# An attention and non-local block in float32: the non-local part of image 6 moved behind the last attention, with other first loads, score banks and tail

One core of a Trainium2 chip. The metric is the device time of one execution in microseconds (us), of the slowest core (here the only one); lower is better. A span in a profile is 1.7 us shorter than the device time of the same run. All runs named here are of the fast state.

## The reference, cut

For each of 8 images x of 512 channels and 32 x 32 = 1024 positions, in float32:

```python
# layer 0: attention, 8 heads of d = 64
q, k, v = (conv1x1(x, W, b).reshape(B, 8, 64, 1024) for W, b in (q, k, v))
attn = softmax(einsum('bhdn,bhdm->bhnm', q, k) * 64 ** -0.5)
x = x + conv1x1(einsum('bhnm,bhdm->bhdn', attn, v).reshape(B, 512, 32, 32), Wp, bp)
# layer 1: non-local block with 256 inner channels, then a norm over the whole batch
g, theta, phi = (conv1x1(x, W, b).reshape(B, 256, 1024) for W, b in (g, theta, phi))
y = einsum('bcd,bdn->bcn', einsum('bcn,bdn->bcd', theta, phi) / 1024, g)
z = conv1x1(y, W_w, W_b) + x
z_hat = (z - mean(z, (0, 2, 3))) * rsqrt(var(z, (0, 2, 3)) + 1e-5)
return z_hat * gamma + beta
```

The norm's mean runs over all images, so no output can be stored before the last z of its channels is known.

## The kernel before

Each image goes through the same stages on TensorE, and their names are those of the PSUM tiles in the profile: pq, pv, pk (projections), ps and po (attention: scores and weighted values), den (softmax denominators), pp (projection of the output), ptp (theta and phi), pf (f = theta phi), pg (g), pwf (f folded into W_w) and pz. The large products are done as seven products of half size (Strassen-Winograd), so they need sums of quarters first: t1 to t4 of the data, w3 to w6 of the weights, on VectorE. The stages overlap, so pq, pv and pk of image b + 1 run between the attention of b and its pp.

PSUM has four slots of two banks; the text calls a slot a bank, as the code does. `free` holds their order. The helpers `pe` and `dve` keep an instruction in program order; a scheduler places everything else, DMA issues too.

```python
    free = ["s0", "s1", "s2", "s3"]
    def next_bank(name):
        free.append(free.pop(0))
        return bank(free[-1], name)

    xt = xp.tile([P, CC, N], F32, tag="x", name="x_0")
    load_w(nc.scalar)                          # quarters of WqT, 256 KB each, on ScalarE's queue
    for h in range(NH):
        for k in range(2):                     # x of image 0 in four pieces of 512 KB
            at = slice(k * CC // 2, (k + 1) * CC // 2), slice(h * 512, (h + 1) * 512)
            nc.sync.dma_start(xt[:, at[0], at[1]], x_v[0, :, at[0], at[1]])

    def join_bias(w):                          # bp += Wp bv, once
        for oc in range(CC):
            m, mc = divmod(oc, CC // 2)
            ps = next_bank(f"pbp_{oc}")
            for c in range(CC):
                ...                            # quarter of Wp
                pe(nc.tensor.matmul(ps[:, 0, :1], quarter[...], bv[:, c:c + 1], ...))
            nc.vector.tensor_tensor(bp[:, oc:oc + 1], bp[:, oc:oc + 1], ps[:, 0, :1], ALU.add)
```

The attention takes 64 steps: 8 units (a pair of heads, half of the positions) of 8 blocks of keys. The weighted values follow the scores by LAG = 2 steps. `acc` sums a unit's exponentials; after four units the four `acc` are spread over one tile by DMA (`spread`), VectorE sums it, one product per half gives the denominators, and their reciprocals go through DRAM (`den_d`) to be broadcast back (`r`). In the last image nothing follows the attention behind which this chain could run, so its units 4 to 7 had a product and a reciprocal each (`normalize_alone`).

```python
        def scores(i):
            ps = bank(tags[i % 2], f"ps_{b}_{u}_{m}")
            ...                                # 4 products, then e = exp(scale * ps) on ScalarE
            if m == NB - 1 and u not in alone: # alone: units 4..7 of the last image
                spread(u)
        def denominators(g, ps):
            columns(ps, folds, lambda j: t[:, 0, j * 512:(j + 1) * 512])
            nc.vector.reciprocal(ri, ps)
            nc.sync.dma_start(d, ri)           # den_d
        def normalize(g, d):
            for i in range(4):
                for j in range(2):
                    nc.sync.dma_start(r[j * D:(j + 1) * D, :], d[row, :].partition_broadcast(D))
                dve(nc.vector.tensor_tensor(part(4 * g + i), part(4 * g + i), r, ALU.mult))
        def normalize_alone(u, ps):
            columns(ps, ones, lambda j: acc[:, j, :])
            nc.vector.reciprocal(ri, ps)
            nc.vector.tensor_tensor(part(u), part(u), ri, ALU.mult)
```

The z of images 0 to 4 wait in DRAM (`spill`). In the last image they are read back (`reload`) while TensorE still works.

Of the kernel before, what the change touches and what calls it, by code (L numbers as in the profile page):

```python
# [16 lines left out]
P = 128  # L17
# [13 lines left out]
def unshifted(ctx: ExitStack, tc: tile.TileContext, a: dict, out: bass.AP):  # L31
# [11 lines left out]
    LATE = 3  # L43
    LAG = 2
# [86 lines left out]
    def weights(name):  # L131

        n, w = loaded.pop(0)
        assert n == name
        if name not in kept:
            weight_sums(w, corner[name])
            kept[name] = dram.tile(list(w.shape), F32, tag=f"kept_{name}", name=f"kept_{name}")
            nc.sync.dma_start(kept[name], w)
        return w

    def join_bias(w):

        for oc in range(CC):
            m, mc = divmod(oc, CC // 2)
            ps = next_bank(f"pbp_{oc}")
            for c in range(CC):
                k, kc = divmod(c, CC // 2)
                quarter = {(0, 0): w[:, 0], (0, 1): w[:, 1], (1, 0): corner["WpT"], (1, 1): w[:, 2]}[m, k]
                pe(nc.tensor.matmul(ps[:, 0, :1], quarter[:, kc, mc * P:(mc + 1) * P], bv[:, c:c + 1],
                                    start=(c == 0), stop=(c == CC - 1)))  # L150
            nc.vector.tensor_tensor(bp[:, oc:oc + 1], bp[:, oc:oc + 1], ps[:, 0, :1], ALU.add)  # L151

    def data_sums(quarters, name, width=2):

        b11, b12, b21, b22 = quarters
        t = [block(f"t{i}_{name}")[:, :width, :] for i in range(4)]
        nc.vector.tensor_tensor(t[0], b12, b11, ALU.subtract)
        nc.vector.tensor_tensor(t[1], b22, t[0], ALU.subtract)
        nc.vector.tensor_tensor(t[2], b22, b12, ALU.subtract)
        nc.vector.tensor_tensor(t[3], b21, t[1], ALU.subtract)  # L160
        return {"11": b11, "21": b21, "22": b22, "t1": t[0], "t2": t[1], "t3": t[2], "t4": t[3]}
# [13 lines left out]
    def seven(name, w, data, positions_out, first, add, between=None, early=False):  # L175



        nk, half = w.shape[2], w.shape[3]
        tags = list(free)  # L180
        free[:] = [tags[3], tags[1], tags[0], tags[2]] if early else [tags[3], tags[1], tags[2], tags[0]]
        slots, begun = {}, set()
        for n, (what, wi, di, s, reads) in enumerate(EARLY if early else SEVEN):
            if s not in slots or early and what == "t4":
                slots[s] = bank(tags[s], f"{name}_{s}_{n}")
                begun -= {one for one in begun if one[0] == s}
            ps, d = slots[s], data[di]
            if positions_out:
                parts = [(ps.rearrange("p h (i f) -> p (h i) f", f=half)[:, i, :], i * half // 512,
                          lambda k, i=i: d[:, k, i * P:(i + 1) * P], lambda k: w[:, wi, k, :])  # L190
                         for i in range(512 // P)]
            else:
                parts = [(ps[:, m, :], m, lambda k, m=m: w[:, wi, k, m * P:(m + 1) * P], lambda k: d[:, k, :])
                         for m in range(half // P)]
            for to_ps, at, lhsT, rhs in parts:
                for k in range(nk):
                    pe(nc.tensor.matmul(to_ps, lhsT(k), rhs(k), start=(s, at) not in begun, stop=(k == nk - 1),  # L197
                                        skip_group_check=True))
                    begun.add((s, at))
            for to, is_first in reads:  # L200
                (first if is_first else add)(to, ps)
            if between and n in between:
                between[n]()
# [15 lines left out]
    load_w(nc.scalar)  # L219
    for h in range(NH):  # L220
        for k in range(2):
            at = slice(k * CC // 2, (k + 1) * CC // 2), slice(h * 512, (h + 1) * 512)
            nc.sync.dma_start(xt[:, at[0], at[1]], x_v[0, :, at[0], at[1]])
# [3 lines left out]
    ones = const.tile([P, D], F32, tag="ones", name="ones")  # L227
# [23 lines left out]
    def heads_of(b, what, w, bias, data, **how):  # L251
# [13 lines left out]
        for c in range(CC):  # L265
            nc.vector.tensor_reduce(peak[:, c:c + 1], t[:, c, :], AX.X, ALU.max, apply_absolute_value=True)
# [30 lines left out]
    def attention(b, q, k, v, near_end):  # L297
# [7 lines left out]
        o = mats.tile([P, CC, N], F32, tag="o", name=f"o_{b}")  # L305
        units = [(p, h) for p in range(NPAIR) for h in range(NH)]
        steps = [(u, m) for u in range(len(units)) for m in range(NB)]
        es, accs, sums, folded = {}, {}, {}, {}
        alone = range(4, 8) if b == B - 1 else ()
        tags = list(free)  # L310

        def part(u):
            p, h = units[u]
            return o[:, p, h * 512:(h + 1) * 512]

        def scores(i):
            u, m = steps[i]
            p, h = units[u]
            ps = bank(tags[i % 2], f"ps_{b}_{u}_{m}")
# [14 lines left out]
            if m == NB - 1 and u not in alone:  # L334
                spread(u)

        def weighted(i):
# [10 lines left out]
            if m == NB - 1:  # L348
                nc.scalar.copy(part(u), ps[:, 0, :])
                nc.vector.tensor_tensor(part(u), part(u), ps[:, 1, :], ALU.add)  # L350

        def spread(u):
# [7 lines left out]
            if i == 3:  # L360
# [3 lines left out]
                for to, l, r in ((t[:, 0], t[:, 0], t[:, 1]), (t[:, 2], t[:, 2], t[:, 3]),  # L364
                                 (folded[g][:, 0], t[:, 0], t[:, 2])):
                    nc.vector.tensor_tensor(to, l, r, ALU.add)
# [11 lines left out]
        def normalize(g, d):  # L378
            for i in range(4):
# [6 lines left out]
        def normalize_alone(u, ps):  # L386
            acc = accs.pop(u)
            columns(ps, ones, lambda j: acc[:, j, :])
            ri = w2.tile([P, 512], F32, tag="ri", name=f"ri_{b}_{u}")
            nc.vector.reciprocal(ri, ps)  # L390
            nc.vector.tensor_tensor(part(u), part(u), ri, ALU.mult)

        for i in range(len(steps) + LAG):
            if i < len(steps):
                scores(i)
            if i == len(steps) - 2:
                near_end()
            if i >= LAG:
                weighted(i - LAG)
            if alone and i in (46, 54, 62):  # L400
                ps = bank(tags[3 - i // 8 % 2], f"psum_{i}")
                if i == 46:
                    d = denominators(0, ps[:, 1, :])
                normalize_alone(i // 8 - 1, ps[:, 0, :])
            if alone and i == 58:
                normalize(0, d)
        free[:] = tags
        if not alone:
            return o, denominators, normalize
        normalize_alone(7, next_bank("psum_7")[:, 0, :])  # L410
        return o, None, None

# [26 lines left out]
    def nonlocal_(b, xt, data, tp, wg, before_wf):  # L439
# [3 lines left out]
        f = w2.tile([P, IC, CI], F32, tag="ri", name=f"f_{b}")  # L443

        def make_f():
            ps = next_bank(f"pf_{b}")[:, 0, :].rearrange("p (c d) -> p c d", c=IC)
            for c in range(IC):
                for i in range(NB):
                    pe(nc.tensor.matmul(ps[:, c, :], tp[:, i, c * P:(c + 1) * P], tp[:, i, CI:],  # L449
                                        start=(i == 0), stop=(i == NB - 1)))  # L450
            nc.scalar.mul(f, ps, 1.0 / N)
# [4 lines left out]
        def first(q, ps):  # L456
            d = int(q[0]) - 1
            nc.scalar.activation(part(q), ps[:, 0, :], AF.Identity, bias=gb[:, d:d + 1])  # L458

        seven(f"pg_{b}", wg, data, False, first,  # L460
              lambda q, ps: nc.vector.tensor_tensor(part(q), part(q), ps[:, 0, :], ALU.add), {5: make_f})
# [74 lines left out]
    def last_z():  # L536
        order = [B - LATE, B - 1, *range(B - LATE + 1, B - 1)]
        begun = None
        for oc in range(CC):
            for n, b in enumerate(order):  # L540
                _, g, wf = late[b]
                ps = next_bank(f"pz_{b}_{oc}")
                for h in range(NH):
                    for d in range(IC):
                        pe(nc.tensor.matmul(ps[:, h, :], wf[:, d, oc * P:(oc + 1) * P], g[d][:, h * 512:(h + 1) * 512],  # L545
                                            start=(d == 0), stop=(d == IC - 1)))
                t = z[b][oc]
                dve(nc.vector.scalar_tensor_tensor(t, ps.rearrange("p h n -> p (h n)"), wb[:, oc:oc + 1], t,
                                                   ALU.add, ALU.add))
                if n == 0 and begun:  # L550
                    finish(oc - 1, *begun)
                for h in range(NH):
                    dve(nc.vector.bn_stats(stats[:, oc, b * NH + h, :], t[:, h * 512:(h + 1) * 512]))
# [24 lines left out]
    data = data_sums(quarters_of(xt), "x_0")  # L578
    q, peak_q = heads_of(0, "q", weights("WqT"), bq, data, early=True)
# [9 lines left out]
    load_w(nc.sync)  # L589
    for b in range(B):  # L590
# [5 lines left out]
        def near_end():  # L596
            if not last:
                nxt["data"] = data_sums(quarters_of(nxt["x"]), f"x_{b + 1}")

        o, denominators, normalize = attention(b, q, k, v, near_end)  # L600
# [12 lines left out]
        else:  # L613
            for i, tag in enumerate("vqk"):
# [26 lines left out]
        nonlocal_(b, xt, data, tp, weights("WgT"), before_wf)  # L641
        load_w(nc.sync)
        if b in spill_g:
            put_away(b)
# [8 lines left out]
    pe(nc.tensor.matmul(ps[:D, :1], ones, good, start=True, stop=True))  # L653
# [213 lines left out]
```

## Time and profile before

| | before |
|---|---|
| device time, 3 runs | 2209.64 us (2209.11 to 2211.08) |
| the profiled run | 2211.32 us, span 2209.6 |
| start of pk of image 0 | 33.2 |
| join_bias to pp, pp to ptp (image 0) | 5.87, 27.13 |
| attention of images 0 to 6, first ps to next pq | 110.54 to 110.59 each |
| pk to pp in images 2 to 5 / 1 / 6 | 24.03 / 24.48 / 24.79 |
| ptp of image 6 to ptp of image 7 | 201.07 |
| last product (count) to the end of the span | 22.1 |

The rows below the third are differences between the starts of a stage's first matmul in TensorE's timeline. This is the way in which all gains below are counted: it takes in waits, cold clock and switching alike. The views themselves stand in the prediction. One more serves as the base of a later comparison, the start of an attention (image 2) in TensorE's timeline (columns: start, duration, engine, line, operation, count, and idle time before it):

```profile
627.55 1.95 PE L324 MATMUL ps<-q,k 64*64 64x512 f32 x16
629.83 1.09 PE L324 MATMUL ps<-q,k 64*64 64x512 f32 x8 [0.33 <-ACT e L327]
630.74 1.04 PE L346 MATMUL po<-e,v 64*64 64x512 f32 x8
```

The third block of scores waits, and po starts 3.19 us after the first score.

### The profile page before, as it was taken

The numbers are of one execution on the slowest core, as the hardware profiler recorded it, in microseconds if no ns is written. First come the engines' busy times: TensorE is split into PE (matmuls) and PEld (weight loads), VectorE is DVE, ScalarE is ACT, GpSimd is POOL, SyncE is SP. The second block draws the span as 40 slices with busy tenths as digits, with TensorE's granted clock in tenths as the row PEclk, the third lists the DMA queues.
The fourth block names the chain that finished last, engine by engine and source line by source line (L and its number), as shares of the span: only waits on it lengthen the run. The fifth ranks groups of instructions, "written<-read, shape, count | busy, mean of one in ns | idle before, by whom it ended". The sixth has DMA issues, their size and how long they took to land.

```text
span 2209.6 us, 28905 instructions
## 1 busy us (share of the span) xinstructions
PE 2166.6 (98%) x12234; PEld 1066.1 (48%) x12234; DVE 1321.1 (60%) x1299; ACT 735.8 (33%) x821; POOL 35.4 (2%) x36
## 2 busy tenths in 40 slices
PE   8999999999999999999999999999999999999996
PEld 3534664346633456335563365633655336643362
DVE  5476546765467644776547755467463765447736
ACT  1463103641046310462105621165203641055215
POOL 0000000000000000000000000000000000000000
PEclk9999999999999999999999999999999999999998
DMA  6212323113131232312223113231334113222347
GB/s 238 77 39 60 126 98 120 39 44 133 60 129 39 60 107 75 116 40 69 96 93 105 40 64 119 90 91 31 108 114 143 39 30 129 79 84 66 129 159 306
DMA packets 58265, 209.07 MB, mean 95 GB/s; under 512 B 10384, under 2 KB 16784, under 8 KB 52752
## 3 DMA queue, kind: packets, MB, share of 16 engines
q1 hardware_dynamic: 56752, 206.09, 28.5%
q8 instruction: 98, 1.61, 0.3%
q10 hardware_dynamic: 1376, 1.05, 0.2%
q14 instruction: 39, 0.32, 0.0%
HBM read 129.12 MB, written 46.53 MB: 79 GB/s over the span
## 4 chain that ended last, share of the span: by engine, by line
PE 93%; DMA 3%; DVE 2%; issue 1%; ACT 1%; SPq 0%; DVEq 0%; ACTq 0%
PE ps L324 19%; PE po L346 19%; PE pp L197 9%; PE pq L197 9%; PE ptp L197 9%; PE pv L197 8%; PE pk L197 6%; PE pg L197 4%; PE pf L449 3%; PE pz L197 2%; DMA r<-den_d 2%; PE pz L545 2%; PE pwf L468 1%; PE den L295 1%; ACT e L327 0%
## 5 line engine op out<-in xcount | busy, mean ns | idle before, releaser
L327 ACT ACTIVATE e<-ps 128x1024 f32<-128x1024 f32 x512 | 523.7, 1024 | 390.7 <-PE ps L324 383.1
L333 DVE TENSOR_TENSOR acc<-acc,e 128x1024 f32<-128x1024 f32 x384 | 470.0, 1224 | 123.7 <-ACT e L327 117.1
L324 PE MATMUL ps<-q,k 64*64 64x512 f32 x4096 | 532.4, 591 | 2.6 <-ACT e L327 2.6
L346 PE MATMUL po<-e,v 64*64 64x512 f32 x4096 | 529.5, 590 | 0.0
L324 PEld LDWEIGHTS ps<-q,k 64*64 64x64 f32 x4096 | 155.0, 133 | 291.6 <-issue 278.9
L346 PEld LDWEIGHTS po<-e,v 64*64 64x64 f32 x4096 | 156.7, 133 | 283.9 <-issue 281.2
L458 ACT ACTIVATE g<-pg,gb 128x512 f32<-128x512 f32 x32 | 22.0, 687 | 434.3 <-PE pg L197 434.3
L331 DVE TENSOR_TENSOR acc<-e,e 128x1024 f32<-128x1024 f32 x64 | 78.2, 1223 | 121.0 <-ACT e L327 87.7
L197 PE MATMUL pk<-t_x,w_WkT 128*128 128x512 f32 x256 | 114.0, 593 | 0.7 <-DVE k L214 0.7
L197 PE MATMUL pv<-w_WvT,t_x 128*128 128x256 f32 x512 | 114.5, 379 | 0.0
L197 PE MATMUL ptp<-w_tp,t_x 128*128 128x256 f32 x512 | 114.4, 379 | 0.0
L197 PE MATMUL pp<-t_o,w_WpT 128*128 128x512 f32 x256 | 113.7, 593 | 0.0
L197 PE MATMUL pq<-t_x,w_WqT 128*128 128x512 f32 x256 | 113.6, 592 | 0.0
L197 PEld LDWEIGHTS ptp<-w_tp,t_x 128*128 128x128 f32 x512 | 97.3, 190 | 13.2
L197 PEld LDWEIGHTS pv<-w_WvT,t_x 128*128 128x128 f32 x512 | 97.2, 190 | 13.2
L197 PE MATMUL pq<-x,w_WqT 128*128 128x512 f32 x192 | 89.7, 612 | 6.3 <-DMA w_WqT<-in_WqT_dram 6.3
L262 ACT ACTIVATE k<-pk,bk 128x512 f32<-128x512 f32 x64 | 40.5, 684 | 165.0 <-PE pk L197 165.0
L384 DVE TENSOR_TENSOR o<-o,r 128x512 f32<-128x512 f32 x60 | 40.8, 689 | 91.0 <-DMA r<-den_d 91.0
L197 PE MATMUL pp<-o,w_WpT 128*128 128x512 f32 x192 | 91.1, 620 | 2.2 <-DVE bp L151 2.2
L278 ACT COPY v<-pv 128x1024 f32<-128x1024 f32 x32 | 32.4, 1012 | 173.6 <-PE pv L197 173.6
L262 ACT ACTIVATE q<-pq,bq 128x512 f32<-128x512 f32 x62 | 39.2, 683 | 146.2 <-PE pq L197 146.2
L197 PE MATMUL pv<-w_WvT,x 128*128 128x256 f32 x384 | 87.5, 381 | 0.0
(132 smaller groups left out, 1947.4 us busy)
## 6 DMA issues: line engine op xcount, KB each, us to landing
fold<-acc SPq DMA_DIRECT2D x240, 128.0 KB, 2.3
x<-in_x_dram SPq DMA_DIRECT2D x32, 512.0 KB, 5.5
r<-den_d SPq DMA_DIRECT2D x120, 128.0 KB, 3.0
w_WqT<-kept_WqT SPq DMA_DIRECT2D x7, 1792.0 KB, 7.4
w_WvT<-kept_WvT SPq DMA_DIRECT2D x7, 1792.0 KB, 7.3
w_WkT<-kept_WkT SPq DMA_DIRECT2D x7, 1792.0 KB, 7.1
w_WpT<-kept_WpT SPq DMA_DIRECT2D x7, 1792.0 KB, 8.7
w_tp<-kept_tp SPq DMA_DIRECT2D x7, 1792.0 KB, 7.3
```

Source lines behind the costliest of these rows:

```text
L197: pe(nc.tensor.matmul(to_ps, lhsT(k), rhs(k), start=(s, at) not in begun, stop=(k == nk - 1), skip_group_check=True))
L262: nc.scalar.activation(t[:, c, cols(q)], ps[:, m, :], AF.Identity, bias=bias[:, c:c + 1])
L278: seven(f"pv_{b}", w, data, True, lambda q, ps: nc.scalar.copy(at(q), as_v(ps)), lambda q, ps: nc.vector.tensor_tensor(at(q), at(q), as_v( ...
L295: pe(nc.tensor.matmul(ps[j * D:(j + 1) * D, :], lhsT, rhs(j), start=True, stop=True, skip_group_check=True))
L324: pe(nc.tensor.matmul(ps[c * P // 2:(c + 1) * P // 2, j, :], k[r, p, keys], q[r, p, h * 512:(h + 1) * 512], start=True, stop=True, skip_gr ...
L327: nc.scalar.activation(e, ps, AF.Exp, scale=SCALE)
L331: nc.vector.tensor_tensor(accs[u], es[u, 0], e, ALU.add)
L333: nc.vector.tensor_tensor(accs[u], accs[u], e, ALU.add)
L346: pe(nc.tensor.matmul(ps[j * D:(j + 1) * D, r, :], v[keys, m, (2 * p + j) * D:(2 * p + j + 1) * D], e[keys, j, :], start=(m == 0), stop=(m ...
L384: dve(nc.vector.tensor_tensor(part(4 * g + i), part(4 * g + i), r, ALU.mult))
L449: pe(nc.tensor.matmul(ps[:, c, :], tp[:, i, c * P:(c + 1) * P], tp[:, i, CI:], start=(i == 0), stop=(i == NB - 1)))
L545: pe(nc.tensor.matmul(ps[:, h, :], wf[:, d, oc * P:(oc + 1) * P], g[d][:, h * 512:(h + 1) * 512], start=(d == 0), stop=(d == IC - 1)))
```

## The change

Intent: give TensorE work to do behind the last attention, so that its denominators can go by four units as in all other images; and trim the start, the score banks, join_bias and the tail. Five parts:

1. **Last image.** pg and pwf of image 6 run after the last attention, pf of image 6 inside it. The last four denominators come behind the fourth of seven groups of pg; `normalize_alone` is gone.
2. **Start.** The first pieces of x and WqT are half as large, and eight products of zeros run first. w3 is made on VectorE between the sums of x, and the matmuls of the first product go chunk by chunk of x. (VectorE's reductions of image 0 for the peaks of q and k are now kept in program order, too.)
3. **Slots.** The third block of scores goes into a third bank.
4. **join_bias** uses one bank and one addition, so that pp has three banks at hand.
5. **Tail.** The last product and its additions go in two halves. Besides, the multiplications with r go in the order 0, 2, 1, 3.

The diff, cut to the lines that matter here:

```diff
+    WARM = 8
 def join_bias(w):
+        ps = next_bank("pbp")[:, 0, :CC]
         for oc in range(CC):
-            ps = next_bank(f"pbp_{oc}")
-                pe(nc.tensor.matmul(ps[:, 0, :1], quarter[...], bv[:, c:c + 1], ...))
-            nc.vector.tensor_tensor(bp[:, oc:oc + 1], bp[:, oc:oc + 1], ps[:, 0, :1], ALU.add)
+                pe(nc.tensor.matmul(ps[:, oc:oc + 1], quarter[...], bv[:, c:c + 1], ...))
+        nc.vector.tensor_tensor(bp, bp, ps, ALU.add)
... start
+    for x_part, w_part in (((0, 1, 0), (w_first[:, 0], 0, 0, 0, 1)), ((1, 2, 0), (w_first[:, 0], 0, 0, 1, 2)),
+                           ((2, 4, 0), ...), ((0, 2, 1), ...), ((2, 4, 1), ...)):
+        nc.sync.dma_start(xt[:, c0:c1, at], x_v[0, :, c0:c1, at])
+        nc.scalar.dma_start(to[:, c0:c1], quarter("WqT", m, k)[:, c0:c1])
+    for i in range(WARM):
+        pe(nc.tensor.matmul(ps[:, :P], warm, warm, start=True, stop=True))
... attention
-            ps = bank(tags[i % 2], f"ps_{b}_{u}_{m}")
+            ps = bank(tags[(0, 1, 3)[i] if i < 3 else (i + 1) % 2], f"ps_{b}_{u}_{m}")
-            if m == NB - 1 and u not in alone:
+            if m == NB - 1 and u == len(units) - 1 and make_f:
+                near_end(lambda: spread(u, dve))
+            elif m == NB - 1:
                 spread(u)
-            for i in range(4):
+            for i in (0, 2, 1, 3):
-            if alone and i in (46, 54, 62):
-                ...
-                normalize_alone(i // 8 - 1, ps[:, 0, :])
+            if make_f and i == 2:
+                make_f(bank(tags[2], f"pf_{b - 1}"))
+            if make_f and i == 46:
+                d = denominators(0, bank(tags[2], f"den_{b}_0")[:, 0, :])
+            if make_f and i == 58:
+                normalize(0, d)
... last image, behind the attention
         else:
+            nonlocal_(b - 1, held["x"], nxt["data"], held["f"], weights("WgT"), lambda: None,
+                      {3: lambda: nxt.update(d=denominators(1, next_bank(f"den_{b}_1")[:, 0, :]))})
+            normalize(1, nxt["d"])
+            load_w(nc.sync)                    # w_tp, 1.8 MB
+            put_away(b - 1)
             for i, tag in enumerate("vqk"):
                 reload(i, mats, tag)           # z of images 0 to 2
... tail
+                halves = ((0, 1), (1, 2)) if (oc, n) == (CC - 1, LATE - 1) else ((0, NH),)
```

## The prediction

> **What bounds the kernel now.** I read the page's busy table first, then what TensorE waited for, then the granted clock in narrow windows, the timeline around each wait, and last the transfers of the tail.
>
> ```profile
> span 2209.6 us, 28905 instructions
> PE 2166.6 (98%) x12234; PEld 1066.1 (48%) x12234; DVE 1321.1 (60%) x1299; ACT 735.8 (33%) x821; POOL 35.4 (2%) x36
> ```
>
> TensorE is the bound: of the span it is idle 43.0 us only. Everything that it waited for (view: waits of PE, in us in total, times, longest):
>
> ```profile
> PE pq L197 <- DMA w_WqT<-in_WqT_dram: 6.3, 1, 6.3
> PE psum L295 <- DVE acc L333: 4.9, 1, 4.9
> PE psum L295 <- DVE ri L373: 3.8, 1, 3.8
> PE ps L324 <- ACT e L327: 2.6, 8, 0.3
> PE pp L197 <- DVE bp L151: 2.2, 1, 2.2
> PE pk L197 <- DVE k L214: 0.7, 2, 0.5
> ```
>
> These are 20.5 us; the other 22 lie behind the last product (2187.5 to 2209.6). The change names nearly all of them. But a busy TensorE isn't always at full clock; the windows of 2 us around the second and fifth wait show it (third last column: the granted clock, before DMA share and GB/s):
>
> ```profile
> 2026.00:2028.00 2.00, 0.00 (x0) 0.00 (x0) 2.00 (x2) 0.00 (x0) 0.00 (x0) 1.00 0.00 0
> 2028.00:2030.00 2.00, 0.27 (x2) 0.27 (x4) 1.68 (x1) 0.00 (x0) 0.00 (x0) 0.79 0.00 0
> 2030.00:2032.00 2.00, 2.00 (x8) 0.33 (x10) 0.25 (x1) 0.00 (x0) 0.00 (x0) 0.50 0.35 131
> 2036.00:2038.00 2.00, 2.00 (x24) 0.70 (x20) 0.97 (x1) 1.02 (x1) 0.00 (x0) 1.00 0.18 67
> ...
> 274.00:276.00 2.00, 2.00 (x3) 0.68 (x2) 1.26 (x2) 0.00 (x0) 0.00 (x0) 0.50 0.00 0
> ```
>
> After a hole of 3.8 us TensorE runs at half clock until 2036, six matmuls in 2 us become three. So a wait costs itself and, if long enough, some 2.5 to 3 us more. The clock column says 1.00 at the start of the span, yet the first 16 matmuls of pq take 9.9 us against 7.03 for the next 16: the start is cold as well, until about 12.2 us.
>
> The tail is another matter:
>
> ```profile
> 2164.00:2168.00 4.00, 4.00 (x10) 1.71 (x9) 3.45 (x4) 4.00 (x5) 0.00 (x0) 1.00 1.02 406
> ```
>
> From there until 2204 every such window shows a DMA share of 1.0 and some 400 GB/s. The outputs are 32 transfers of 512 KB, 16.8 MB, at 404 GB/s 41.5 us: from the first output (2162.75) on, the stores set the end, not the arithmetic.
>
> **What the Trainium skill says.** (1) "TensorE: Matmul & The Clock Gate", Part 1: the array clock halves after an idle window of about 3.4 us and is full again after about that long of sustained work, the window running freely. The trace agrees on the first (half clock 2.9 to 3.4 us after the last dense matmul in two places), while getting warm took 5.2 to 6.6 us here. (2) The same page, "Architectural detail: the array is 16× 32×32": VectorE and ScalarE take their instructions strictly in order; here the wait for bp is of that kind, a 0.16 us addition behind 4.59 us of reductions for peak_k. (3) "DMA: Bandwidth & Descriptors", "Queues, rings and completion order": on each DMA engine descriptors of one queue are consumed in order. The chain of before agrees: a broadcast r issued 0.6 us after a 1.8 MB weight load took 9.43 us instead of the usual 3.0:
>
> ```profile
> 1849.79 0.58 SPq L125
> 1850.37 0.04 issue
> 1850.41 9.43 DMA r<-den_d
> ```
>
> **The change part by part.**
>
> *Start.* The first pieces shrink from 512 + 256 KB to 256 + 128 KB, and eight products of zeros warm the clock meanwhile. By 6.25 us some 1.27 MB had moved (10 GB/s, 236, 348 in the windows of 2 us); if both queues share, the first pieces are down when 512 KB have moved, at 4.2 us. The zeros start at about 1.1 us; a warm-up of 5.9 us (mean of before) ends at 7.0. So 2.8 us of real work run cold, then 6.4 of the first eight products at 0.86 us: the third group, s1t1, starts at 12.5, where before it started at 16.03. It needs w3 = a21 + w2; a21 landed at 11.2 and the addition takes 0.7, so 12.0: just in time. **Gain 3.5** (2.3 to 4.5).
>
> *Attention starts.* Each begins ps, ps, then waits for the first exp because there are two banks; the third bank takes that away, 2.6 us in all. The bank is the one that the stage before used last, and its evacuation ends about when step 2 wants it: I count **2.2**.
>
> *join_bias.* Before, the four products went through all four banks, and pp had to wait for the bank that VectorE read late. Now one bank serves, pp uses the three others: 2.24 us saved. The 3.2 us of one-column products (266.7 to 269.9) stay and hardly count as work for the clock, so the cold run behind (8 matmuls in 6.46 us against 3.44: 2.9) goes with a chance of six in ten. **Gain 4.0** (2.2 to 5.1).
>
> *Last attention.* Before: from 1945.22 to the first pp at 2074.10 is 128.9 us; the attention of image 6 takes 110.6 (1688.52 to 1799.11). The difference of 18.3 is two waits (8.7), five denominator products (6.9, two of them cold), and 2.7 of cold ps and po between 2031.6 and 2036.3. The pp behind takes 25.67 against 24.14, cold again: 1.5. Together **19.8** over a plain attention.
>
> After, with T the end of the last po. The order of instructions shows pg in seven groups of 1.72, den behind the fourth (T+6.9), the three other groups, pwf (3.4), pp 11 (3.4), pp 21.
> - pf stands before the first po and uses po's bank, so po waits for f's evacuation: 0.2 + 0.60 + 0.2 = **1.0**, a wait that wasn't there; changing the tile form adds 0.2.
> - VectorE comes to T with a backlog: four multiplications with r (0.69 each) and two waits for r lie among the last six additions. Last exp at T-1.4; I get the last acc at T+1.9 (image 6 before: T+3.2). The fold lands 3.05 later (as before, 1802.27 to 1805.32): 5.0. Three additions and one g between: 3 x 1.2 + 0.7, so T+9.3. den wanted to start at 6.9: **wait 2.4**.
> - den ends at T+10.3; behind t2 and t3 of x VectorE starts the reciprocal at 11.5, 3.35; den_d is written in 2.4: T+17.3. But on the queue the 1.8 MB of w_tp, free when pg ends (T+15.5), stand between den_d and r. They land after 7.3, at T+22.9, r some 1.3 later as in the chain above, multiplication 0.7: T+25.0. pp 21 wants it at T+22.3: **wait 2.8**. The t1 of o, which needs the last two r, is then late by **0.6**.
> - Two denominator products, 0.93 each: **1.9**.
> - Each of the two holes is a little short of those that made the clock drop; a quarter of a chance each for some 2.5: **1.0** with rounding.
>
> Sum 9.9 in place of 19.8: **gain 9.9** (6 to 13). pg, pwf and f are the same work as before, only elsewhere.
>
> *Tail.* Halving the last product lets VectorE start earlier: STT and statistics 0.7 + 0.64 for each half end at about 2189.7 in place of 2190.14, 0.45 us. The stores are behind by then (share 1.0 without a gap), so it gains **0**. What moves the first store moves the end, and all gains above do.
>
> *The rest.* The order 0, 2, 1, 3 of the multiplications can touch the 0.7 us of pk's waits: 0.
>
> Sum 3.5 + 2.2 + 4.0 + 9.9 = 19.6: 2209.6 - 19.6 = **2190 us**, 0.9% less.
>
> **The rivals.**
> *A: the waits change places.* The den of the last four units and the broadcast r behind w_tp cost as much as what was removed. For it: the in-order queue above, and that fold of image 6 was summed at T+9.9, so even the plain chain doesn't fit in 6.9. Against: pg and pwf give 15 us of work behind which the chain runs. With both holes at 5 us and both cold, the last attention gains only 2 to 3: about 2197.
> *B: everything hides.* The fold lands early, r lands before w_tp is through, no cold stretch: the last attention gains 15, the bias 5.1, the start 4.5: about 2183.
> *C: the end is held by the stores.* If their start were bound by loads of z and g and not by TensorE, nothing would come through and the time would stay at about 2209. Against: the DMA share is 0.0 to 0.1 from 2152 to 2164, just before the stores, so nothing is queued there and they start with the arithmetic.
>
> **Range and chances.** A and B span 2183 to 2197, and the start alone adds 1 us either way; that is my range for 8 in 10. For 2% faster 44 us would have to go; idle and cold time outside the tail are about 21 + 11, so it can't. Slower by 2% would need a new hole of 60 us: none in the order of instructions.
>
> **What would show it.** Right: first pq at about 4.2, s1t1 at 12.5; the waits of ps for e gone; no wait of pp for bp; in the last image new waits of TensorE for f (1), for fold in front of den (2.4) and for o<-o,r in pp (2.8), no reciprocal of psum; r with a landing of 7 us or more just behind w_tp; from first store to end 47 us as before. Wrong: pp 21 without a wait, or den without one; a half clock behind join_bias; a span from first to last store that shrinks.

## The result, and the profile after

**2194.01 us** (6 runs, 2193.32 to 2194.64) against **2209.38 us** before (6 runs, 2207.88 to 2211.08). The ratio is 0.993 (95% interval 0.9917 to 0.9943). A ratio here is the mean of one kernel's fast runs over that of the other's of the same rounds, so not quite the ratio of the medians. The time fell by 15.4 us where 19.6 were predicted; it lies in the range, and is within 2% as said.

```profile
span 2192.0 us, 28926 instructions
PE 2158.6 (98%) x12238; PEld 1069.6 (49%) x12238; DVE 1320.3 (60%) x1304; ACT 733.7 (33%) x820; POOL 35.4 (2%) x36
```

What TensorE waited for now (same columns as in the prediction):

```profile
PE pp L203 <- DVE o L405: 3.1, 1, 3.1
PE den L314 <- issue: 2.4, 1, 2.4
PE pk L203 <- DVE k L220: 1.8, 1, 1.8
PE pq L203 <- DVE w_WqT L609: 1.7, 1, 1.7
PE warm_ps L240 <- DVE warm L226: 1.1, 1, 1.1
PE pg L203 <- DVE t_x_again L159: 0.8, 1, 0.8
PE po L365 <- ACT f L456: 0.7, 1, 0.7
```

All six waits of before but that of pk are gone, and the three that the prediction announced in the last image are there: 3.1 (said 2.8), 2.4 (2.4) and 0.7 (1.0). Two came unannounced, those of pg and pq. (The row of warm_ps is the wait for the zeros at the very start. Where a row ends in "issue", the view found nothing that the engine waited for; den starts 0.10 us after VectorE's last sum of fold, so that is its wait.) The spans of the two profiles differ by 17.6 us; the stage starts say where:

| stage (us) | before | after | gain | predicted |
|---|---|---|---|---|
| start to pk of image 0 | 33.20 | 31.02 | 2.2 | 3.5 |
| attentions 0 to 6 | 7 x 110.58 | 7 x 110.03 | 3.9 | 2.2 |
| join_bias to pp | 5.87 | 3.49 | 2.4 | 4.0 with the next |
| pp to ptp, image 0 | 27.13 | 26.04 | 1.1 | |
| pk to pp, images 1 and 6 | 49.27 | 50.16 | -0.9 | 0 |
| ptp of image 6 to that of 7 | 201.07 | 192.79 | 8.3 | 9.9 |
| after the last product | 22.1 | 21.4 | 0.7 | 0 |
| sum (of unrounded gains) | | | 17.6 | 19.6 |

The profiled run of before happens to be 1.9 us slower than the median (2211.32 against 2209.38) and that after is 0.3 faster than its own, which accounts for 17.6 against 15.4.

The start of the same attention (image 2) in TensorE's timeline, to be held against the three lines of before:

```profile
622.54 2.81 PE L341 MATMUL ps<-q,k 64*64 64x512 f32 x24
625.16 1.04 PE L365 MATMUL po<-e,v 64*64 64x512 f32 x8
```

Three blocks of scores run without a gap, and po starts after 2.62 us, not 3.19: 0.57 gained, though the row of waits had named 0.33. The timeline has matmuls running into the idle time, since their ends are modelled; start to start is the safer measure.

The clock around join_bias (windows of 2 us, columns as in the prediction). The one-column products run until 267.5, then pp:

```profile
265.50:267.50 2.00, 2.00 (x20) 2.00 (x20) 2.00 (x3) 0.00 (x0) 0.00 (x0) 1.00 0.99 306
267.50:269.50 2.00, 2.00 (x5) 0.92 (x6) 2.00 (x3) 0.00 (x0) 0.00 (x0) 0.71 0.22 73
269.50:271.50 2.00, 2.00 (x4) 0.85 (x3) 1.41 (x4) 0.00 (x0) 0.00 (x0) 0.50 0.00 0
```

The wait for bp is gone, the half clock isn't. And the tail, where the stores fill the queue (DMA share 1.02, 406 GB/s), long after the last product (2170.6):

```profile
2183.00:2187.00 4.00, 0.00 (x0) 0.00 (x0) 0.00 (x0) 0.00 (x0) 0.00 (x0) 0.50 1.02 406
```

From the first store (2145.89) to the end are 46.1 us, before 46.8. The stores themselves take as long as before: the last of the 32 lands 44.40 us after the first was issued, before 44.38. The 0.7 us lie behind it, from the last landing to the end of the program: 1.7 us against 2.4.

In the last image the chain of work that ended last runs from the last acc to pp (start, duration, what; engine names with q are sequencers):

```profile
2035.50 1.24 DVE acc L350
...
2037.34 2.30 DMA fold<-acc
...
2042.72 1.23 DVE fold L387
...
2046.21 3.28 DVE ri L394
...
2049.51 2.65 DMA den_d<-ri
...
2052.70 6.79 DMA r<-den_d
```

With T = 2033.43 (the end of the last po, where pg starts), the last acc ends at T+3.3 (predicted T+1.9), den starts at T+10.6 (9.3), den_d has landed at T+18.7 (17.3) and r is multiplied in at T+26.9 (25.0). The whole chain is late by what its first link is late, while TensorE, held up by 0.8 us in front of pg, comes to it late too. That is why the waits came out nearly right: both sides of each subtraction were late by about as much (den at T+10.6 and not 9.3, TensorE ready for it at T+8.2 and not 6.9). That the first is 2.4 to the digit is luck.

### The profile page after: what moved, and what is told of

Read it like the earlier page. It is cut to its first block, busy times and chain, and to the rows that moved or that the text cites. A ratio compares the mean times of both kernels' runs of the same rounds, so it can differ in the third digit from the quotient of the medians.

```text
span 2192.0 us, 28926 instructions
## 1 busy us (share of the span) xinstructions
PE 2158.6 (98%) x12238; PEld 1069.6 (49%) x12238; DVE 1320.3 (60%) x1304; ACT 733.7 (33%) x820; POOL 35.4 (2%) x36
## 4 chain that ended last, share of the span: by engine, by line
PE 95%; DMA 2%; DVE 1%; ACT 1%; issue 0%; SPq 0%; DVEq 0%
PE ps L341 20%; PE po L365 20%; PE ptp L203 9%; PE pp L203 9%; PE pv L203 9%; PE pq L203 9%; PE pk L203 8%; PE pg L203 4%; PE pf L454 3%; PE pz L203 2%; PE pz L569 2%; PE pwf L489 1%; DMA r<-den_d 1%; PE den L314 1%; ACT z L598 0%; DMA x<-in_x_dram 0%
```

## The experiments

The 12 kernels ran in three calls, each on one chip and with its own runs of before (medians 2210.07, 2209.71, 2207.34 us); 5 rounds each, so 4 or 5 runs per kernel. All results were correct. The intervals of a ratio are 0.0025 to 0.003 wide (6 us), so single terms of 1 or 2 us are read from the stages of the profiles, and the times only bear them out.

| kernel | median us | ratio to before | ptp 6 to ptp 7 |
|---|---|---|---|
| after | 2194.01 | 0.993 | 192.79 |
| r ahead on the queue (x_rfirst) | 2193.94 | 0.9925 | 192.25 |
| multiplications earlier (x_norm) | 2193.54 | 0.9926 | 193.07 |
| r ahead, z late (x_zlate) | 2189.0 | 0.991 | 189.85 |
| both (x_zlnorm) | 2184.4 | 0.9891 | 186.13 |
| both, f and w3 too (x_best) | 2183.97 | 0.989 | 184.58 |
| den one group later (x_den4) | 2195.06 | 0.9944 | 195.63 |
| f later (x_pf) | 2192.02 | 0.9929 | 195.3 |
| tail not halved (x_tail) | 2194.6 | 0.9928 | 192.4 |
| two score banks (x_bank2) | 2197.93 | 0.9945 | 192.73 |
| join_bias in four banks (x_bias4) | 2195.97 | 0.994 | 192.14 |
| one product of zeros (x_warm1) | 2192.88 | 0.9924 | 194.42 |
| old order of multiplications (x_order) | 2194.43 | 0.9937 | 193.76 |

### Is it w_tp that holds r?

Edit: r of the last four units, then w_tp and the spill of g, pinned in this order on the queue of SyncE.

```diff
-            dma.dma_start(w, kept[name])
+            sp(dma.dma_start(w, kept[name]), name == "tp" and len(queue) == 1)     # sp: keep in program order
-                    nc.sync.dma_start(r[...], d[row, :].partition_broadcast(D))
+                    sp(nc.sync.dma_start(r[...], d[row, :].partition_broadcast(D)), b == B - 1 and g)
```

> The changed kernel with one thing more: on the transfer queue the eight broadcasts r of the last four denominators go ahead of the 1.8 MB load of w_tp and of the spill of g. Theory (r is late because it stands behind w_tp in the queue): r lands some 3 us after den_d in place of 6.8 us and more, TensorE's wait for o<-o,r in front of pp 21 (3.1 us) and the half clock behind it (1.7 us) vanish, the time falls by 4 to 5 us, and w_tp still lands before ptp. Rival (r is late because den_d itself lands late, or the broadcast takes as long anyway): the wait stays at 2 us or more, the time within 1 us of the changed kernel.

Measured: pp's wait fell from 3.1 to 2.2 us, no more, and the time did not move (2193.94). The queue of SyncE shows why; another transfer took w_tp's place:

```profile
2047.24 0.32 SPq L400 DMA_DIRECT2D den_d<-ri  x1
2047.60 0.94 SPq L551 DMA_DIRECT2D z<-spill  x2
2050.02 2.40 SPq L408 DMA_DIRECT2D r<-den_d  x4
```

The slowest r landed in 5.1 us (after: 6.9). VectorE then did two evictions of pp before the multiplication, at 2056.43. So taking w_tp away is not enough: the next loads in line, two of z (512 KB each, issued at 2047.60 and 2048.08, landed at 2052.81 and 2054.72), took its place. In the changed kernel itself w_tp was the one transfer ahead of r: the last load of z before it had landed at 2051.49, r was issued at 2052.17. What I had overlooked is what follows w_tp in the queue.

### The loads of z held back

Edit: as above, and `reload` of images 0 to 3 pinned behind.

```diff
-            nc.sync.dma_start(t[:, cc, :], spill[b][:, cc, :])
+            sp(nc.sync.dma_start(t[:, cc, :], spill[b][:, cc, :]), b < 4)
```

> The loads of z that stood ahead of r are issued only after r, w_tp and the spill of g (nothing else differs from the run that put r ahead of w_tp). Theory, the queue as a whole holds r: r is issued some 2.8 us after den_d, lands 3.0 us after its issue instead of 6.4, so TensorE's wait in front of the second group of pp falls from 2.2 to under 0.5 and the cold stretch behind goes; from ptp of image 6 to ptp of image 7 some 189 us instead of 192.25, the time near 2190. Rival, the delay is in the broadcast or in den_d itself: landing stays above 5 us, wait near 2.2, time near 2194.

Measured: 2189.0 us. The queue, and the first multiplication with r in VectorE's timeline:

```profile
2045.49 0.33 SPq L400 DMA_DIRECT2D den_d<-ri  x1
2047.55 7.01 SPq L408 DMA_DIRECT2D r<-den_d  x8
```

```profile
2051.26 0.69 DVE L409 TENSOR_TENSOR o<-o,r 128x512 f32<-128x512 f32 x1 [1.38 <-DMA r<-den_d]
```

No r took over 3.3 us. pp waits for nothing any more, its clock stays full, and from pp to ptp it is 24.20 us instead of 29.00. One reservation: the scheduler now also put the multiplications ahead of the two evictions of pp, so part of the 2.2 us against the run before is VectorE's order. The landing itself, 5.1 to 3.3, is the queue's. Against the run before, the stage gained less than pp to ptp did (2.4 us of 4.1), because this run went cold behind the wait for den: from den to pp 11.26 us, not 9.7.

### VectorE's backlog at the end of the attention

Edit, alone, then with the two above:

```diff
-            if make_f and i == 58:
+            if make_f and i == 52:
                 normalize(0, d)
```

> The changed kernel with the four multiplications by r of the first four units placed six steps earlier in the last attention (step 52 in place of 58). Theory (VectorE carries a backlog from these multiplications and their waits over the end of the attention): the last acc ends near the end of the last po in place of 3.3 us behind it, the wait of pg for t_x (0.8 us) goes and the wait of den (2.4 us) falls below 1 us; time 2 to 3 us lower, unless r is then late behind w_tp by the same clock and takes part of it back as a longer wait of pp. Rival (the fold transfers and additions alone are longer than the work of TensorE beside them): den still waits for 2 us or more.

Measured alone: 2193.54 us. The last acc ends at about T, the wait of pg for the sum of x is gone, and yet den waits 2.4 us:

```profile
2038.27 1.23 DVE L387 TENSOR_TENSOR fold<-fold 128x1024 f32<-128x1024 f32 x1 [2.42 <-DMA fold<-acc]
```

VectorE now stands waiting for the fold transfer, issued at 2032.89, only 2.3 us behind 1 MB of loads of z. From that issue to the first sum it took 5.4 us, not the 3.0 of the changed kernel, where the loads had had 5.7 us to get through. Most of the gain went back into this wait: den starts at T+9.6, not T+10.6. The rest went into the clock: behind den's wait this run lost it (half clock from 2043.0 to 2046.4), the changed kernel had not.

> As the run before it, and the first four multiplications with r six steps earlier, so that VectorE has no backlog at the end of the attention. Theory: with no z load ahead the fold lands in 3.0 us, not 5.4; last acc ends near T, fold additions near T+7.3, so den waits at most 0.7 instead of 2.4, and the wait for the sum of x (0.8) is gone; from ptp to ptp some 186.5 us, the time near 2187. Rival, the fold transfer takes 5 us whatever stands ahead: den waits 2 or more and the time is that of the run before.

Measured together: **2184.4 us**. den waits 0.5 us and pg not at all:

```profile
PE pp L207 <- DVE t_o L164: 0.8, 1, 0.8
PE po L369 <- ACT f L460: 0.7, 1, 0.7
PE den L318 <- PE pg L207: 0.5, 1, 0.5
```

ptp to ptp takes 186.13 us (expected 186.5). The early multiplications are worth 0 while the loads of z stand ahead, and 3.7 us of the stage when they don't; 1.6 of these are the half clock behind den's wait (den to pp takes 9.70 us here, 11.26 in x_zlate).

### Are den's and pp's waits two costs or one?

My sum added them. Edit: den one group of pg later, so TensorE has 1.7 us more to do before it.

```diff
-                      {3: lambda: nxt.update(d=denominators(1, ...))})
+                      {4: lambda: nxt.update(d=denominators(1, ...))})
```

> The products of the last denominators behind the fifth group of pg instead of the fourth, so TensorE has 1.7 us more to do before them. Theory: den's wait and pp's lie on one chain (fold, sum, den, reciprocal, den_d, r), which doesn't start earlier: den waits 0.7 instead of 2.4, pp waits 1.7 to 2.4 us more than the 3.1 of the changed kernel, time 2194 to 2194.8. Rival: the waits are separate costs, as my sum added them: 1.7 gained, 2192.3.

Measured: 2195.06 us, nothing gained:

```profile
PE pp L203 <- DVE o L405: 6.0, 1, 6.0
...
PE den L314 <- PE pg L203: 0.7, 1, 0.7
```

1.7 less in front of den, 2.9 more in front of pp. den starts as late after the last po as before, T+10.7 against T+10.6: both are waits on the same chain, which starts with the last acc and ends with r, and work moved ahead of den only moves the wait. That pp loses more than den gains has two other causes: VectorE now does one addition of g ahead of the reciprocal (0.7), and w_tp (issued at 2045.58) now stands ahead of den_d, too. From the chain that ended last (start, duration, what):

```profile
2046.76 7.74 DMA den_d<-ri
```

In the changed kernel den_d took 2.65 us and r the 6.9, here den_d 7.74 and r 3.4; so this edit changed the order of the queue as well. A sum of waits is right for the time that passes, but not for what it saves to remove one of them.

### f

Edit: pf at step 4, into the bank that the third block of scores has left.

```diff
-            if make_f and i == 2:
-                make_f(bank(tags[2], f"pf_{b - 1}"))
+            if make_f and i == 4:              # after weighted(i - LAG)
+                make_f(bank(tags[3], f"pf_{b - 1}"))
```

> f's products two steps later, into the free bank, so that po need not wait for f's evacuation; everything else as changed. My term says 1.0: 2193.0 against 2194.0; from the start of the last attention to the first pg 118.3 us instead of 119.2. Rival: what is saved there is lost again at the den, whose chain over VectorE doesn't begin earlier: den wait 3.1, time 2194.

Measured: 2192.02 us; by the ratio (0.9929 against 0.993) no difference. The wait for f is gone and the attention to pg takes 118.46 us instead of 119.21. But den's wait stays at 2.4, and more half clock fell into this run (den to pp 11.35 us instead of 9.70, pp to ptp 30.31 instead of 29.00): ptp to ptp 195.3. So 0.75 us saved in its place; whether it reaches the end here is inconclusive.

### The tail

```diff
-                halves = ((0, 1), (1, 2)) if (oc, n) == (CC - 1, LATE - 1) else ((0, NH),)
+                halves = ((0, NH),)
```

> The changed kernel with the last product whole again. Theory (stores set the end): time and the stretch from the first store to the end as in the changed kernel within 0.3 us. Rival (the halves brought the 0.7 us by which that stretch shrank): 0.5 to 0.8 us slower, the stretch 46.8 us again.

Measured: 2194.6 us, and from the last product to the end 21.4 us as in the changed kernel. The halving gains nothing, as predicted: the stores set the end. The 0.7 us that the profile of before is longer there lie behind the landing of the last store (2.4 us to the end there, 1.7 in all 13 other traces, this one included). What makes them is not shown.

### Three score banks

```diff
-            ps = bank(tags[(0, 1, 3)[i] if i < 3 else (i + 1) % 2], f"ps_{b}_{u}_{m}")
+            ps = bank(tags[i % 2], f"ps_{b}_{u}_{m}")
```

> The changed kernel with two banks for the scores at the start of each attention, as before. By the waits of the profile of before it should lose 0.28 us per attention, 2.0 us over seven, by the stretches from attention to pq of the two traces 0.55 us per attention, 3.9 us. The wait of ps for e comes back. In the last image nothing should change, since pf stands between.

Measured: 2197.93 us, 3.9 more than after by the medians (3.3 by the ratios, whose intervals overlap). An attention takes 110.58 us again, and the wait is back:

```profile
PE ps L341 <- ACT e L344: 2.5, 8, 0.3
```

8 x 0.55 = 4.4 by the stages, 3.3 to 3.9 by the time; the row of waits says 2.5. It is eight attentions, not seven: against what I expected the last one loses as well, 119.73 us from its first score to pg instead of 119.21. The term was mis-sized because I took it from that row.

### join_bias

Edit: four banks again.

> join_bias through four banks again, everything else as changed. My prediction's term says 4.0 (2.24 of wait + part of a cold run of 2.9): about 2198. From the stage starts of the two profiles (pbp to pp 5.87 against 3.49, pp to ptp 27.13 against 26.04) I would now say +3.5: 2197.5. Rival: only the wait counts and the cold run comes either way: +2.2, 2196.2; the wait of pp for bp (2.2) is back in all cases.

Measured: 2195.97 us, 2.0 more; join_bias to pp takes 5.77 us again, and the row is back:

```profile
PE pp L203 <- DVE bp L153: 2.2, 1, 2.2
```

That is the rival's number, though the time alone, with 6 us of interval, could not tell it from mine; the stages do. The cold run comes in this kernel too (25.89 us from pp to ptp). But does it come from join_bias? The 12 runs with one bank there (11 experiments and the changed kernel) have the same instructions up to that place, but for the start (two), the score banks (one) and the order of the multiplications (one). In eight pp takes 25.9 to 26.04 us, in four 24.34. One of the four (x_zlate), just behind the same products, where the changed kernel has 0.71:

```profile
266.60:268.60 2.00, 2.00 (x6) 0.96 (x6) 2.00 (x3) 0.00 (x0) 0.00 (x0) 1.00 0.17 59
```

The clock stays at 1.00. In windows of 0.25 us the half clock of the changed kernel lasts from 268.3 to 271.7 and again from 2060.3 to 2063.7, 3.4 us both; in x_zlate from 2039.9 to 2043.3; in x_den4, behind the 6 us hole, 6.8 (2056.5 to 2063.3); in the kernel before 6.8 as well (2029.2 to 2036.0). So it comes in pieces of 3.4 us. One piece costs 26.04 - 24.34 = 1.70 us where TensorE has work throughout, half of 3.4.

Whether the products of join_bias cause one depends on where they fall; here 8 times in 12. The traces show where. In the clock records of each of the 14 traces all changes of the clock lie whole multiples of 3.413 us apart, from the first to the last; so the span divides into fixed windows of this length. Two of them at join_bias, in x_tail and x_zlate, with the instructions of pp alone (TensorE's busy time stands behind the length of the window):

```profile
263.81:267.22 3.41, 1.22 (x3) 0.68 (x4) 0.00 (x0) 1.00 0.71 227
264.97:268.38 3.41, 1.85 (x5) 0.92 (x6) 0.00 (x0) 1.00 0.60 193
```

The rest of both is products of join_bias. Behind the first the clock is halved, behind the second it isn't. In all eight cold runs the window before the drop holds 0.1 to 1.2 us of other products, in the four warm ones the emptiest holds 1.57 to 1.68. The same border divides the waits: leaving out the products of join_bias, a window at full clock with at most 1.36 us of work was always followed by half clock, one with 1.41 or more never but once (1.51, at the last product of before). So this was a matter of phase, and a wait of 2.4 us is enough if most of it falls into one window: of the ten traces with this wait in front of den, five lost the clock there (x_zlate, x_norm, x_pf, x_warm1, x_order), five didn't.

### The zeros at the start

```diff
-    WARM = 8
+    WARM = 1
```

> One product of zeros instead of eight. The first 16 matmuls should take 9.9 us again, not 7.46, and end at 14.5. Theory: the third group waits for w3 until 13.75 anyway, because the second half of x lands at 11.9, so all but some 0.8 to 1.5 us of the 2.4 are hidden: near 2195. Rival: the whole 2.4 is lost: 2196.5 or more.

Measured: 2192.88 us, so nothing lost. The start of the changed kernel in TensorE's timeline, then that of this one:

```profile
1.06 3.78 PE L240 MATMUL warm_ps<-warm 128*128 128x128 f32 x16 [1.06 <-DVE warm L226]
4.64 7.46 PE L203 MATMUL pq<-x,w_WqT 128*128 128x512 f32 x16
13.75 2.41 PE L203 MATMUL pq<-t_x,w_WqT 128*128 128x512 f32 x5 [1.65 <-DVE w_WqT L609]
```

```profile
4.28 8.64 PE L203 MATMUL pq<-x,w_WqT 128*128 128x512 f32 x16 [2.41 <-DMA w_WqT<-in_WqT_dram]
12.75 3.60 PE L203 MATMUL pq<-t_x,w_WqT 128*128 128x512 f32 x8
```

The zeros make the first 16 matmuls 1.2 us faster (not 2.4, as I expected), and then the third group waits for w3. What sets the start is when the second half of x lands, the fourth of its five pieces. In the changed kernel's profile that was late (11.85; then VectorE made t1 and, behind it, w3, until 13.70). Over the 11 kernels with the same start pk began between 29.53 and 31.02, mean 29.95: 3.2 us earlier than in the one profile of before, not 2.2. In each of them that is 19.2 to 19.3 us behind this landing, which scatters from 10.35 to 11.85.

### The order of the multiplications

Edit: 0, 1, 2, 3 again in all images but the last.

> Multiplications with r in the order 0, 1, 2, 3 again, but for the last image. My term says 0: 2194. Rival: the new order makes the wait of pk in image 1 (1.8 us in the changed kernel's profile, 0.1 to 1.8 in the six others): then from pk to pp of image 1 it takes under 24.5 us here and the time is 2192.5.

Measured: 2194.43 us; pk to pp of image 1 takes 25.29 us. The new order isn't the cause of pk's wait: with the old one pk waits 2.6 us in three images. In x_zlate, with the new order, image 1 takes 24.10. In every trace with such a wait one r of 9.4 to 10.7 us, issued behind a weight load, comes before it; the wait scatters from run to run.

### A better version

r ahead, z late, early multiplications, f as tried, and one thing more, w3 ahead of t0:

```diff
-    for to, l, r, op in ((t[0], b12, b11, ALU.subtract), (w[:, 3], a21, w[:, 2], ALU.add),
+    for to, l, r, op in ((w[:, 3], a21, w[:, 2], ALU.add), (t[0], b12, b11, ALU.subtract),
```

> The candidate: r ahead, z late, first multiplications six steps earlier, and besides f's products two steps later in the bank that is free (its wait of 0.7 in front of po goes) and w3 = a21 + w2 ahead of t0 (up to 0.6 at the start). Theory: both are on the path, so 1.0 to 1.4 us less than the run with the first three alone (2184.4): 2183.2. Rival: the start depends on when x lands and scatters by more than this; then the time stays within 2183 to 2186 and only the wait of po in the trace tells.

Measured: **2183.97 us** (2181.64 to 2185.41), ratio 0.989 (0.9875 to 0.9905), against 0.9891 for the run without f and w3. Its interval and that of the changed kernel (0.9917 to 0.9943) don't overlap: it beats both kernels, by 23 and some 9 us. f's wait is gone and ptp to ptp is at 184.58, but in this run pk waited 1.7 us and join_bias was one of the cold ones. pk of image 0 began 18.6 us behind the landing of x's second half, not 19.2, which is the 0.6 expected of w3. So of the two additions only the removed waits are shown, not a time. The gain over the changed kernel is that of x_zlnorm.

## Why the prediction was right, and where it was not

**Right in class and range, and in the waits that it named**, 4 us short in size. Its mechanism was wrong for the zeros and for the clock, and luck helped the sum: the attentions gave 1.7 us more than said, which hides part of what the other terms gave less. Of its own signs of being wrong one came, the half clock behind join_bias. Term by term:

- *Start, 3.5*: 2.2 in the profile pair, 3.2 on the mean of 11 kernels. pq at 4.64 (said 4.2). The step that failed is "just in time": s1t1 was to start at 12.5 and started at 13.75, since the second half of x landed late and w3 stands behind t1 on VectorE. And the warm-up gave nothing (x_warm1: pk at 29.94 without it). There pq starts 2.0 us earlier than before (4.28 against 6.29), which fits the smaller first pieces, and its first 16 matmuls take 1.3 less (8.64 against 9.90), since the full clock came 3.1 us behind the first of them, before 5.6; that is phase again. No run undoes the smaller pieces or the order of the sums alone, so how they share the gain is not shown.
- *Attention starts, 2.2*: 3.9 for seven images by the stages, 3.3 to 3.9 by the time of undoing it (x_bank2). The term was mis-sized by reading a wait row in place of start to start.
- *join_bias, 4.0*: 3.5 in the profile pair; 2.0 by undoing it. The wait was right (2.2 to 2.4). The cold run, which I gave a chance of six in ten to go, stayed in 8 of 12 runs. What it costs was mis-sized as well: it comes in pieces of 3.4 us at half clock, so 1.7 us each. The 2.9 of before were most of two pieces. (The working's 6.46 - 3.44 is 3.0, not 2.9; from pp to ptp it was 27.13 - 24.34 = 2.8.)
- *Last attention, 9.9*: 8.3 in the profile pair, and 193.1 on the mean of the five kernels with the same code there (after, x_tail, x_bias4, x_warm1, x_order), so 8.0. Announced waits: 0.7, 2.4 and 3.1 against 1.0, 2.4 and 2.8. Not announced: pg's wait for the sum of x (0.8), because the last acc ended at T+3.3, not T+1.9: two waits for r, 2.09 and 1.08 us, stood among the last additions. And the cold run behind pp's wait came as a whole piece, 1.7, where the allowance for both holes was 1.0. The step that failed there is "a little short of those that made the clock drop; a quarter of a chance each": in these five kernels six of the ten holes cost a piece.
- *Tail, 0*: right (x_tail). *The rest, 0*: right on the whole (x_order); pk's waits are noise of some 1 us.
- Readings of the working: the windows said to stand around "the second and fifth wait" show the third (ri, 3.8 us) and the fifth; behind the second (4.9 us) the clock was halved as well, from 2070.1 to 2077.0. Some of its times stand 0.07 us off the view (1945.22 for 1945.15), all by the same, so the differences hold.

Of the rivals, A (the waits change places) holds in kind: den and r are the new waits, and x_den4 shows the one grow when the other is filled. Its size, both holes at 5 us, did not come. B (everything hides) needed r ahead of w_tp and of the loads of z, and the earlier multiplications; x_zlnorm, 2184.4, is about B's 2183. C is refuted for the whole and right for the halved tail. On the cause of r's delay the prediction was right, w_tp stood ahead of it (6.9 us, said 7 or more); what it didn't see is that loads of z take this place when w_tp leaves it (x_rfirst against x_zlate).

## What to carry to other kernels

When a short latency chain (a reduction through DRAM, a broadcast) runs beside bulk loads on one queue, pin the chain's transfers ahead and all the bulk behind: here one bulk load moved out of the way gave 0, all of them with an earlier start of the chain 9 us. Waits along one chain are one cost: find its first link (here VectorE's backlog), and don't fill the waits one by one. Take the worth of a wait from start to start of the stages, and count a lost clock in whole pieces, here 1.7 us each; a wait shorter than a piece can cost one.

## What the Trainium skill lacked or had wrong

- "TensorE: Matmul & The Clock Gate", Part 1, says that the window runs freely at 3.4 us and the clock takes two states. The runs agree: the half clock lasted 3.4 or 6.8 us, at 0.50 or 1.00 where a window lies wholly in one state, and its changes lie multiples of 3.413 us apart. It doesn't say how much work keeps a window busy, nor that narrow products hardly count: the one-column products of join_bias fill TensorE's row (2.00 of 2.00 us) and yet the clock fell behind them in 8 of 12 runs; without them the border lay near 1.4 us of work in 3.41. My reading in the prediction, that getting warm takes 5.2 to 6.6 us, was two windows taken for one ramp. The page's "don't fit to a specific cold count" is borne out: with the same start the full clock came between 3.98 us (x_bank2) and 7.01 us (x_rfirst).
- "DMA: Bandwidth & Descriptors", "Queues, rings and completion order", gives the order of descriptors on a ring but not its price to a short transfer: r of 128 KB landed in 3.1 us (the changed kernel's median), up to 5.1 behind loads of z (x_rfirst), 6.9 with w_tp ahead, and up to 10.65 behind weight loads elsewhere in the changed kernel; a fold of 128 KB behind loads of z in 4.7 to 5.1 (x_norm) instead of 2.3.
- "Trainium Architecture — The Big Picture", "What this means for kernel authors", gives some 360 GB/s of HBM per core. The tail ran at 406 GB/s for tens of us. "Perfetto Trace Analysis", "Roofline", has it right for a core alone (a ceiling of about 435).
